# Layer 2 FFN results in a four-layer Macaron transformer kernel: update and norm of each sequence entered at set ticks of the next stage

## The chip, the cores and the metric

The kernel runs on one core of a Trainium2 chip. The metric is the device time of one execution in microseconds (us), as the median of several runs. All arithmetic is fp32. The engines are called as in the profile: PE (TensorE), DVE (VectorE), ACT (ScalarE), POOL (GpSimd) and SP (SyncE, which only issues transfers here).

## The reference

The input x holds 4 sequences of 512 tokens with 128 features. There are four layers, each a half-weighted FFN, an attention and the same FFN again, every one of them fed with a layer norm without weights:

```python
x = x + 0.5 * _L2_ffn_ref(_layernorm(x), L2_ffn_router_w, ...)
x = x + _L2_attn_ref(_layernorm(x), L2_attn_Wqkv, L2_attn_Wout)
x = x + 0.5 * _L2_ffn_ref(_layernorm(x), L2_ffn_router_w, ...)
x = x + 0.5 * _L3_ffn_ref(_layernorm(x), L3_ffn_wqkv, ...)
```

The layer 2 FFN is a mixture of eight experts: a router picks one expert for each token, which runs a gated two-layer network. The layer 2 attention has 16 heads and works in blocks. The layer 3 FFN is itself a small transformer of two layers with local attention over windows. The change lies at the two borders "first layer 2 FFN to layer 2 attention" and "second layer 2 FFN to layer 3 FFN", with a smaller piece at the first layer 0 FFN.

## The kernel before

x and y (the normed x) lie in SBUF as 128 tokens by 16 tiles by 128 features, four tiles (TB) to a sequence b. yT holds y turned, 128 features by 512 tokens for each sequence.

**Norms as chains.** The norm of a sequence has three parts. `statistics` (L196) makes four pairs of bn_stats and bn_aggr on DVE (L202, L205) and then `inverse_root`, eight small dependent operations (L184 to L190). `scaled` (L209) writes y in four operations (L214). `turn` (L236) has PE transpose the four tiles into a PSUM bank (`pt_y`, L161) and ACT copy it to yT (L241). So that this work needn't stand in one block, the kernel keeps chains. `chain(b)` opens a list for sequence b, and what is put into it is a part with a gap. `tick()`, which the loops of a stage call between their own parts, moves a clock on by one, and runs the next part of each chain whose gap has passed since the part before it. `leave_normed(b, spare, gap)` (L266) puts statistics, scale and, after a further gap, turn into a chain. `take(b)` (L289) runs what is left of b's chain at once and says whether y of b is ready; `begin_sequence(b)` (L297) is take, or else the whole norm on the spot.

**Order.** `tc.keep_in_program_order` pins an instruction among the pinned ones of its engine; the others are placed by a scheduler, which knows the dependencies and its own estimates of durations. Matmuls, transposes and many ACT instructions are pinned. In the kernel before, update, statistics and scale of the layer 2 FFN are not.

**Layer 2 FFN** (`l2_ffn`, L1211). The tokens are sorted into slots of 128, one expert for each slot, and the slots run through PE, ACT and DVE in a software pipeline; each slot's result is sent to a DRAM table od. Then, for each sequence, four indirect transfers issued on POOL fetch the rows of its tokens from od into y (L1327), and `update` (L1329, the DVE instruction is L1331) adds half of y to x. Update goes into the chain with gap 0, and leave_normed follows with gap 2. The tile pool of the stage is given back when all 16 transfers have landed, and the first tiles of the next stage are placed in that memory.

**Layer 2 attention** (`l2_attn`, L1351). A loop over n runs from -9 to 19, four n for each sequence; a table says at which n the parts of a sequence stand: stat at -9, scale at -8 and features (turn) at -7 ahead of the sequence's first n, each asking `take(b)` first, then projections k and q (`first` writes t at L1377, `second` at L1383), the keys km (L1394), the values v (L1409) and, from 0 on, scores s (L1429), their maximum (L1434) and a subtraction on POOL (L1435). The loop ticks once for each n below 0 and five times for each n from 0 on.

**Layer 3 FFN** (`l3_ffn`, L1549). Eight units (two inner layers by four sequences) of four steps each. A step projects q and k (`p_qk`, PE) and v, squares p_qk on ACT (sq), turns q and k by angle on DVE (t at L1611 and L1614), sums squares (rn, L1616), and on POOL adds the two t (L1618), takes an inverse root and scales (L1619). Later parts of a step run 2 to 6 steps behind: features, scores and their maximum (L1664, L1666), exponentials on ACT, products with sums on POOL (L1681), values. sq and the second t have one buffer each. `norm_unit` and `open_unit` fetch the sequence's norm two and one step ahead of a unit, and the loop, which begins at n = -2, ticks six times for each n.

**Layer 0 FFN** (`l0_ffn`, L331) ends with four updates of x (L479) out of one PSUM bank, which run one after the other.

Of the kernel before, what the change touches and what calls it, by code (L numbers as in the profile page):

```python
# [25 lines left out]
ALU = mybir.AluOpType  # L26
# [3 lines left out]
B, S, D, H, HD = 4, 512, 128, 16, 8  # L30
# [73 lines left out]
def tile_macaron(ctx, tc, x_in, const_in, vec_in, w0_in, ws_in, ws3_in, w2f_in, w3_in, out):  # L104
    nc = tc.nc
# [16 lines left out]
    def bank(tag, name):  # L122
        n = 2 if tag in "kqd" else 1
        return psum["pool"].tile([P, n * 512], F32, tag=tag, name=name, bufs=psum["bufs"][tag])

    x = keep.tile([P, NT, D], F32, name="x")
# [26 lines left out]
    y = keep.tile([P, NT, D], F32, name="y")  # L153
# [3 lines left out]
    def mm(dst, lhsT, rhs, start=True, stop=True):  # L157
        nc.tensor.matmul(dst, lhsT=lhsT, rhs=rhs, start=start, stop=stop)
# [7 lines left out]
    def transpose_in_order(dst, src):  # L166
        tc.keep_in_program_order(transpose(dst, src))
# [5 lines left out]
    def rows(ap, n):  # L173

        return ap[:, None, :].to_broadcast([ap.shape[0], n, ap.shape[1]])

    def inverse_root(sb, dst, src, name, op, c, eng=None):


        n = src.shape[-1]  # L180
        v = sb.tile([P, 3, n], F32, tag=name, name=name, bufs=2)
        eng = eng or nc.vector
        xx, yy, t = (v[:, i, :] for i in range(3))
        eng.tensor_scalar(xx, src, c, None, op)  # L184
        eng.tensor_scalar(yy.bitcast(I32), xx.bitcast(I32), -0.5, float(0x5F1FFFF9), ALU.mult, ALU.add)
        for to, a, b in ((yy, -0.703952253, 1.681913895), (dst, -0.50000016, 1.50000048)):
            eng.tensor_mul(t, yy, yy)
            if eng is nc.vector:
                eng.scalar_tensor_tensor(t, t, a, xx, ALU.mult, ALU.mult)
                eng.scalar_tensor_tensor(to, t, b, yy, ALU.add, ALU.mult)  # L190
            else:
                eng.tensor_mul(t, t, xx)
                eng.tensor_scalar(t, t, a, b, ALU.mult, ALU.add)
                eng.tensor_mul(to, t, yy)

    def statistics(src, b, eng=None, pinned=False):  # L196

        st = keep.tile([P, TB, 6], F32, tag="ln_st", name="ln_st", bufs=2)
        mv = keep.tile([P, TB, 2], F32, tag="ln_mv", name="ln_mv", bufs=3)
        r = keep.tile([P, TB], F32, tag="ln_r", name="ln_r", bufs=3)  # L200
        for t in range(TB):
            first = nc.vector.bn_stats(st[:, t, :], src[:, b * TB + t, :])  # L202
            if pinned and t == 0:
                tc.keep_in_program_order(first)
            nc.vector.bn_aggr(mv[:, t, :], st[:, t, :])  # L205
        inverse_root(keep, r, mv[:, :, 1], "ir4", ALU.add, 1e-5, eng)
        return mv, r

    def scaled(dst, src, b, stats):  # L209

        mv, r = stats
        for t in range(b * TB, b * TB + TB):
            i = t - b * TB
            nc.vector.tensor_scalar(dst[:, t, :], src[:, t, :], mv[:, i, 0:1], r[:, i : i + 1], ALU.subtract, ALU.mult)  # L214


    ordered = {"act": False}
# [1 line left out]
    def by_order(i):  # L219
        if ordered["act"]:  # L220
            tc.keep_in_program_order(i)
# [11 lines left out]
    def normalize(dst, src, b, pinned=False):  # L233
        scaled(dst, src, b, statistics(src, b, None, pinned))

    def turn(b):  # L236

        pt = bank("m", "pt_y")
        for t in range(TB):
            transpose_in_order(pt[:, ts(t, P)], y[:, b * TB + t, :])  # L240
        by_order(nc.scalar.copy(yT[:, b, :], pt))  # L241
# [6 lines left out]
    def chain(b):  # L248
        parts = deque()
        chains.append([b, clock[0], parts])  # L250
        return lambda gap, f, products=True: parts.append((gap, f, products))
# [11 lines left out]
                busy |= c[2][0][2]  # L263
                run(c)

    def leave_normed(b, spare, gap):  # L266

        st = []
        spare(1, lambda: st.append(statistics(x, b)), False)

        def scale():
            scaled(y, x, b, st[0])
            ready.add(b)

        spare(1, scale, False)
        spare(gap, lambda: turn(b))
        if routed:
            spare(1, lambda: logits(b))
# [4 lines left out]
    def finish_chains(b=None):  # L283
        while any(b in (None, c[0]) for c in chains):
            for c in reversed(list(chains)):
                if b in (None, c[0]):
                    run(c)

    def take(b):  # L289

        finish_chains(b)
        if b in ready:
            ready.discard(b)
            return True
        return False
# [32 lines left out]

    def l0_ffn(tag):  # L331
        with pool(tag) as sb:
            acc = sb.tile([P, 2, 4, 32], F32, name="acc")
            agg = sb.tile([64, 32], F32, name="agg")
# [139 lines left out]
            pb = bank("m", "pb")  # L474
            for b in range(B):
                mm(pb[:, ts(b, D)], selb[:, ts(b, P)], o4)
            for b in range(B):
                xb = x[:, ts(b, TB), :]
                nc.vector.scalar_tensor_tensor(xb, rows(pb[:, ts(b, D)], TB), 0.5, xb, ALU.mult, ALU.add)  # L479

# [718 lines left out]
    def logits(b):  # L1201

        nc.sync.dma_start(yd.rearrange("(p t) d -> p t d", t=NT)[:, ts(b, TB), :], y[:, ts(b, TB), :])
        pl = bank("m", "pl2")
        for t in range(TB):
            mm_in_order(pl[:, ts(t, 8)], yT[:, b, ts(t, P)], WS(ws, "2f_rw"))
        nc.vector.tensor_add(
            routed["g"][:, ts(b, TB), :], pl[:, : TB * 8].rearrange("p (t e) -> p t e", e=8), rows(VEC(vec, "2f_rb"), TB)
        )

    def l2_ffn(tag):  # L1211
        ready.clear()
        with pool(tag) as sb, banks(tag + "ps", a=2, g=2, t=2, m=2):
            l2_slots(sb)

    def l2_slots(sb):
        od = dram.tile([P * SLOTS, D], F32, tag="od", name="od")
        g = routed.pop("g")
        softmax8(sb, g)
# [4 lines left out]
        src = oh  # L1224
        for i in range(4):
            n, dst = 1 << i, cum[i % 2]
            nc.vector.tensor_copy(dst[:, :n, :], src[:, :n, :])
            nc.vector.tensor_add(dst[:, n:, :], src[:, n:, :], src[:, : NT - n, :])
            src = dst
# [95 lines left out]
        for b in range(B):  # L1325
            for i in range(b * TB, b * TB + TB):
                nc.gpsimd.indirect_dma_start(y[:, i, :], None, od[:, :], bass.IndirectOffsetOnAxis(ap=at[:, i : i + 1], axis=0))  # L1327

            def update(b=b):  # L1329
                xb, yb = x[:, ts(b, TB), :], y[:, ts(b, TB), :]  # L1330
                nc.vector.scalar_tensor_tensor(xb, yb, 0.5, xb, ALU.mult, ALU.add)  # L1331

            spare = chain(b)
            spare(0, update, False)
            leave_normed(b, spare, 2)

# [12 lines left out]
    def l2_attn(v4s):  # L1351
        pin = tc.keep_in_program_order
        with pool("l2a") as sb:
            stats, four, qk, kms, steps, ao, aoT = {}, {}, {}, {}, {}, {}, {}

            def stat(b):
                stats[b] = None if take(b) else statistics(x, b)

            def scale(b):
                if stats[b]:  # L1360
                    scaled(y, x, b, stats[b])

            def features(b):
                if stats[b]:
                    turn(b)

            def repeated(b):

# [105 lines left out]
            def output(b):  # L1474
# [6 lines left out]


            parts = [
                (stat, -9, 3), (scale, -8, 3), (features, -7, 3), (repeated, -4, 4),
                (lambda b: first(b, "k"), -6, 4), (lambda b: second(b, "k"), -5, 3),
                (lambda b: first(b, "q"), -5, 4), (lambda b: second(b, "q"), -4, 3),
                (lambda b: keys(b, (0, 1)), -4, 4), (lambda b: keys(b, (2, 3)), -3, 3),
# [5 lines left out]
            for n in range(-9, NT + 4):  # L1493
                for place, (part, lag) in enumerate(stages):
                    if part and 0 <= n - lag < NT:
                        part(n - lag)
                    for f, at, when in parts:
                        b, rest = divmod(n - at, TB)
# [333 lines left out]
    with pool("ws") as wp:  # L1832
        ws = wp.tile([P, WS.n], F32, name="ws")
        nc.sync.dma_start(ws, ws_in)
        with banks("ps0"), pool("l0x") as sb:
            tiles = attention0_tiles(sb)
            l0_ffn("l0f")
            l0_attn(tiles)
            l0_ffn("l0g")
        w3 = keep.tile([P, WA], F32, tag="wa", name="w3")  # L1840
        nc.sync.dma_start(w3[:, : W3.n], w3_in)
        with pool("l2x") as l2x:
            with pool("l1x") as xb:
                tiles, vms = attention_tiles(xb), linear_tiles(xb)
                v4s = attention2_tiles(l2x)
                for n in "wb":
                    nc.gpsimd.tensor_scalar_mul(VEC(vec, f"ln2{n}"), VEC(vec, f"ln2{n}"), 0.5)
                l1_ffn("l1f", xb, tiles)
                l1_attn(vms)
                routed["g"] = l2x.tile([P, NT, 8], F32, tag="g2f", name="g2f")  # L1850
                l1_ffn("l1g", xb, tiles)
                with banks("ps1", e=6, m=2):
                    finish_chains()
            l2_ffn("l2f")
            with banks("ps2"):
                routed["g"] = l2x.tile([P, NT, 8], F32, tag="g2f", name="g2f")
                l2_attn(v4s)
                finish_chains()
            l2_ffn("l2g")
    l3_ffn(w3, "l3f", True)  # L1860
    l3_attn()
    l3_ffn(w3, "l3g", False)
# [145 lines left out]
```

## Time and profile before

| what | value |
|---|---|
| median of 3 runs | 2889.82 us (2889.73 to 2892.66) |
| profiled execution | 2886.26 us; its span 2884.6 us |
| mean granted PE clock | 0.871 |
| PE, DVE, ACT, POOL busy | 78%, 62%, 43%, 32% of the span |
| first layer 2 FFN's gathers, first update to last | 1365.16 to 1380.21 us |
| first and second group of attention scores (L1429) | 1401.40 and 1409.99 us |
| end of layer 2 attention (last update of x, L1479) | 1499.70 us |
| second layer 2 FFN's gathers, first update to last | 1609.48 to 1624.31 us |
| layer 3 FFN: first p_qk on PE, first t (L1611) on DVE | 1633.33 and 1638.18 us |
| layer 3 FFN: L1618 of steps 0, 3, 5 and 10 on POOL | 1640.74, 1661.08, 1675.80, 1719.30 us |

The times in the rows are starts, counted from the start of the profiled execution's span. A line of a timeline gives start, duration, engine, source line, operation, what it writes and reads with shapes, how many equal ones are drawn together, and in brackets how long the engine had idled before it and what ended the wait. A line of windows gives, for a stretch, the busy time of each engine with its number of instructions, the granted PE clock as a share of full speed, and the share and rate of transfers.

### The profile page before, as it was taken

How to read it: one execution, taken by the hardware profiler on the slowest of the kernel's cores; microseconds unless marked ns; L12 is line 12 of the kernel's file. 1: busy time of each engine (PE TensorE's matmuls, PEld its weight loads, DVE VectorE, ACT ScalarE, POOL GpSimd, SP SyncE). 2: the span in 40 equal slices, each digit the busy share in tenths (PEclk: the TensorE clock that was granted, in tenths of full speed). 3: DMA queues.
4: the chain of work that ended last, by engine and by line, in shares of the span. 5: the costliest groups of instructions: out<-in, count | busy, mean ns of one | idle time of the engine just before them, and what ended most of it. 6: DMA issues, size and time to landing. Idle time of an engine off the chain costs nothing. (4 is left out here: it accounts for less than half of the span.)

```text
span 2884.6 us, 46981 instructions
## 1 busy us (share of the span) xinstructions
PE 2245.8 (78%) x17562; PEld 1171.8 (41%) x17562; DVE 1788.8 (62%) x4844; ACT 1243.1 (43%) x2678; POOL 911.9 (32%) x1704
## 2 busy tenths in 40 slices
PE   4387448988678899758668578997789998789987
PEld 2154123333343333347458455555322222455553
DVE  4745576775675677544754577776356554777763
ACT  3154214433333433313423277776134444567763
POOL 1022012233121231213313486774100000777661
PEclk8578659999887999869868799999689999899998
DMA  3052010000000000027007210000000000110000
GB/s 135 11 158 67 0 59 1 1 1 1 1 1 1 1 1 5 4 75 257 9 16 272 72 25 19 22 21 8 0 1 1 1 1 1 26 23 21 22 20 12
DMA packets 33772, 99.14 MB, mean 34 GB/s; under 512 B 6184, under 2 KB 12072, under 8 KB 33032
## 3 DMA queue, kind: packets, MB, share of 16 engines
q1 hardware_dynamic: 30616, 88.03, 9.4%
q0 software_dynamic: 2496, 5.12, 0.8%
q8 instruction: 139, 2.28, 0.3%
q10 hardware_dynamic: 432, 2.98, 0.3%
q14 instruction: 89, 0.73, 0.1%
HBM read 66.88 MB, written 14.55 MB: 28 GB/s over the span
## 5 line engine op out<-in xcount | busy, mean ns | idle before, releaser
L802 ACT ACTIVATE PT<-pk_at 128x1024 f32<-128x1024 f32 (+3 forms) x384 | 310.8, 809 | 543.9 <-PE pq_at L164 470.6
L164 PE MATMUL pk_at<-qx,km 32*128 32x512 f32 (+3 forms) x1536 | 368.1, 556 | 61.3 <-ACT PT L802 56.3
L164 PE MATMUL po_at<-PT,vh 128*32 128x512 f32 (+3 forms) x1536 | 328.7, 510 | 4.4 <-POOL PT L805 4.2
L772 DVE CUSTOM_DVE_ANT_0 s<-pq_at,cst 128x384 f32<-128x384 f32 (+3 forms) x512 | 248.4, 485 | 97.2 <-PE pq_at L164 85.8
L1563 ACT ACTIVATE s<-s,nm,rn 128x128 f32<-128x128 f32 x512 | 245.5, 482 | 2.1 <-DVE nm L1669 1.9
L805 POOL TENSOR_SCALAR_AFFINE_SELECT PT<-PT 128x256 f32<-128x256 f32 x256 | 106.8, 419 | 411.5 <-ACT PT L802 411.4
L164 PE MATMUL pq_at<-km,qT 32*128 32x384 f32 (+3 forms) x1024 | 225.2, 528 | 13.7 <-DVE nm L772 7.3
L164 PEld LDWEIGHTS pk_at<-qx,km 32*128 32x128 f32 x1536 | 119.7, 189 | 266.2 <-ACT PT L802 206.7
L767 DVE TENSOR_REDUCE nm<-pq_at 128x2 f32<-128x1024 f32 x128 | 156.2, 1225 | 104.4 <-PE pq_at L164 103.9
L1618 POOL TENSOR_TENSOR t<-t,t 128x1024 f32<-128x1024 f32 x64 | 151.3, 2364 | 132.1 <-DVE t L1614 131.7
L161 PE MATMUL pt_y<-ident,y 128*128 128x128 f32 x224 | 55.1, 376 | 157.6 <-DVE y L214 118.4
L164 PE MATMUL p_qk<-w,hT 128*128 128x512 f32 x256 | 146.5, 701 | 11.0 <-DVE t L1614 9.1
L164 PE MATMUL pq_at<-km,t 32*128 32x512 f32 x512 | 149.4, 689 | 7.0 <-DVE nm L767 4.9
L164 PEld LDWEIGHTS po_at<-PT,vh 128*32 128x32 f32 x1536 | 55.7, 109 | 222.2 <-issue 144.0
L161 PE MATMUL pt<-ident,s 128*128 128x128 f32 x640 | 92.2, 291 | 62.8 <-POOL s L1681 36.7
L241 ACT COPY yT<-pt_y 128x512 f32<-128x512 f32 x56 | 32.7, 584 | 242.8 <-PE pt_y L161 242.7
L1681 POOL TENSOR_TENSOR s<-s,sm 128x1024 f32<-128x1024 f32 x64 | 121.4, 1897 | 49.3 <-DVE sm L1680 41.2
L1611 DVE TENSOR_TENSOR t<-p_qk,w 128x1024 f32<-128x1024 f32 x64 | 78.3, 1223 | 71.7 <-ACT sq L1563 71.4
L1563 ACT ACTIVATE sq<-p_qk 128x1024 f32<-128x1024 f32 x64 | 65.5, 1023 | 127.7 <-PE p_qk L164 76.0
L161 PEld LDWEIGHTS pt<-ident,s 128*128 128x128 f32 x640 | 77.5, 149 | 95.2 <-POOL s L1681 51.5
L161 PEld LDWEIGHTS pt_y<-ident,y 128*128 128x128 f32 x224 | 35.0, 173 | 188.3 <-issue 119.0
L1305 DVE SCALAR_TENSOR_TENSOR hT<-pa,w,sg 128x128 f32<-128x128 f32 x184 | 51.8, 344 | 84.8 <-ACT sg L1304 63.7
(428 smaller groups left out, 5145.3 us busy)
## 6 DMA issues: line engine op xcount, KB each, us to landing
w<-in_w2f_dram SPq DMA_DIRECT2D x46, 836.0 KB, 5.9
vb<-v SPq DMA_DIRECT2D x112, 128.0 KB, 2.2
skew<-qe SPq DMA_DIRECT2D x16, 512.0 KB, 3.0
rel<-skew SPq DMA_DIRECT2D x64, 128.0 KB, 3.3
w<-in_w_dram SPq DMA_DIRECT2D x1, 4147.0 KB, 12.4
w<-in_w_dram SPq DMA_DIRECT2D x1, 3200.0 KB
od<-o SPq DMA_DIRECT2D x46, 64.0 KB, 5.0
yd<-y SPq DMA_DIRECT2D x8, 256.0 KB, 2.3
```

Source lines behind the costliest of these rows:

```text
L161: return nc.tensor.transpose(dst, src, ident[: src.shape[0], : src.shape[0]])
L164: tc.keep_in_program_order(nc.tensor.matmul(dst, lhsT=lhsT, rhs=rhs, start=start, stop=stop))
L241: by_order(nc.scalar.copy(yT[:, b, :], pt))
L767: nc.vector.tensor_reduce(to, pq.rearrange("p (i n) -> p i n", i=2), AX.X, ALU.max)
L772: nc.vector.tensor_tensor_reduce(s[:, :nk], pq[:, i * 512 : i * 512 + nk], causal[:, S - nk :], 1.0, -BIG, ALU.add, ALU.max, nm[:, qt, at ...
L802: by_order(nc.scalar.activation(PT[:, :, q0:], pk[:, :, q0:], AF.Exp, scale=SC8))
L805: nc.gpsimd.affine_select(d, d, pattern=[[0, 2], [1, P]], base=0, channel_multiplier=-1, compare_op=ALU.is_ge, fill=0.0)
L1305: nc.vector.scalar_tensor_tensor(hT[s][:, c, :], pa[:, ts(c, P)], b1[:, c : c + 1], sg, ALU.add, ALU.mult)
L1563: tc.keep_in_program_order(nc.scalar.activation(*args, **kw))
L1611: nc.vector.tensor_mul(by_head(t1), by_head(p3), over(tab[:, 0]))
L1618: nc.gpsimd.tensor_add(t1, t1, t2)
L1681: nc.gpsimd.tensor_mul(s, s, bcast(sm, P))
```

## The change

- The layer 2 FFN takes a tuple `ticks`. Update of sequence b enters its chain with gap ticks[b]: (0, 5, 8, 13) for the first FFN, (0, 13, 36, 60) for the second, where all were 0.
- Update and the four y operations of these chains are pinned in program order on DVE.
- The transfers of all sequences are issued in a loop of their own, ahead of the loop that makes the chains. Their order stays.
- The attention's stat, scale and features are replaced by one begin_sequence at -7.
- The first layer 0 FFN puts the updates of sequences 1 to 3 into their chains with gaps 2, 3 and 4; the second stays as it was.

```diff
-    def scaled(dst, src, b, stats):
+    def scaled(dst, src, b, stats, pinned=False):
...
-            nc.vector.tensor_scalar(dst[:, t, :], src[:, t, :], mv[:, i, 0:1], r[:, i : i + 1], ALU.subtract, ALU.mult)
+            s = nc.vector.tensor_scalar(dst[:, t, :], src[:, t, :], mv[:, i, 0:1], r[:, i : i + 1], ALU.subtract, ALU.mult)
+            if pinned:
+                tc.keep_in_program_order(s)
...
-    def leave_normed(b, spare, gap):
+    def leave_normed(b, spare, gap, pinned=False):
...
-            scaled(y, x, b, st[0])
+            scaled(y, x, b, st[0], pinned)
...
-    def l0_ffn(tag):
+    def l0_ffn(tag, chained):
...
-            for b in range(B):
+            def update(b):
                 xb = x[:, ts(b, TB), :]
                 nc.vector.scalar_tensor_tensor(xb, rows(pb[:, ts(b, D)], TB), 0.5, xb, ALU.mult, ALU.add)
+            for b in range(B):
+                if b and chained:
+                    chain(b)(b + 1, lambda b=b: update(b), False)
+                else:
+                    update(b)
...
+        for b in range(B):
             def update(b=b):
                 xb, yb = x[:, ts(b, TB), :], y[:, ts(b, TB), :]
-                nc.vector.scalar_tensor_tensor(xb, yb, 0.5, xb, ALU.mult, ALU.add)
+                tc.keep_in_program_order(nc.vector.scalar_tensor_tensor(xb, yb, 0.5, xb, ALU.mult, ALU.add))
             spare = chain(b)
-            spare(0, update, False)
-            leave_normed(b, spare, 2)
+            spare(ticks[b], update, False)
+            leave_normed(b, spare, 2, True)
...
             parts = [
-                (stat, -9, 3), (scale, -8, 3), (features, -7, 3), (repeated, -4, 4),
+                (begin_sequence, -7, 3), (repeated, -4, 4),
...
-            l0_ffn("l0f")
+            l0_ffn("l0f", True)
...
-            l0_ffn("l0g")
+            l0_ffn("l0g", False)
...
-            l2_ffn("l2f")
+            l2_ffn("l2f", (0, 5, 8, 13))
...
-            l2_ffn("l2g")
+            l2_ffn("l2g", (0, 13, 36, 60))
```

In the built order of the changed kernel, b0's norm still stands ahead of the next stage's own work. On DVE in the attention, b1's block stands behind the first k product, b2's and b3's around the first group of scores and ahead of the second group. In the layer 3 FFN, b1's stands between steps 0 and 1, b2's in steps 4 and 5, b3's in steps 8 and 9, and PE has the transposes of each ahead of the following step's p_qk.

More of the change, by code (lines that the diff above doesn't have):

```diff
@@ L1209, in logits, with l2_ffn, l2_slots @@
         )
-    def l2_ffn(tag):
+    def l2_ffn(tag, ticks):
         ready.clear()
         with pool(tag) as sb, banks(tag + "ps", a=2, g=2, t=2, m=2):
-            l2_slots(sb)
-    def l2_slots(sb):
+            l2_slots(sb, ticks)
+    def l2_slots(sb, ticks):
         od = dram.tile([P * SLOTS, D], F32, tag="od", name="od")
@@ L1353, in l2_attn @@
         with pool("l2a") as sb:
[L1354 to L1365, printed above, removed]
+            four, qk, kms, steps, ao, aoT = {}, {}, {}, {}, {}, {}
             def repeated(b):
```

## The prediction

> **What bounds the kernel now.** I read the page, then the idle time in front of the changed line L1331, then VectorE's timeline on both sides of it, then the windows of the stages that follow. The page says how much each engine does, and nothing of where:
>
> ```profile
> PE 2245.8 (78%) x17562; PEld 1171.8 (41%) x17562; DVE 1788.8 (62%) x4844; ACT 1243.1 (43%) x2678; POOL 911.9 (32%) x1704
> ```
>
> No engine is full over the span, so the two places must be read by themselves. L1331 is the update x += y/2; its idle time over both layer 2 FFNs:
>
> ```profile
> L1331 DVE SCALAR_TENSOR_TENSOR x<-y,x x8: 691/692/693, 1365.2 to 1624.3; 128x512 f32<-128x512 f32 x8
> its engine sat idle before it (us, times) until:
>   DMA y<-od,at: 26.0, 8
> ```
>
> All of it is a wait for gathers, which the change does not touch. VectorE around the first FFN's end (start, duration, instruction, idle before it and what ended that):
>
> ```profile
> 1375.05 0.69 DVE L1331 SCALAR_TENSOR_TENSOR x<-y,x 128x512 f32<-128x512 f32 x1 [2.79 <-DMA y<-od,at]
> ...
> 1376.01 1.19 DVE L214 TENSOR_SCALAR y<-x,ln_mv,ln_r 128x128 f32<-128x128 f32 x4
> ...
> 1380.21 0.69 DVE L1331 SCALAR_TENSOR_TENSOR x<-y,x 128x512 f32<-128x512 f32 x1 [3.00 <-DMA y<-od,at]
> ...
> 1386.63 1.11 DVE L214 TENSOR_SCALAR y<-x,ln_mv,ln_r 128x128 f32<-128x128 f32 x4
> 1387.66 0.68 DVE L1377 TENSOR_TENSOR t<-p,cst 128x512 f32<-128x512 f32 x1
> ```
>
> Between the last update (1380.21) and the attention's first own operation (1387.66) lie 7.45 us of norms of sequences that are not needed yet: that is what can be won. At the second FFN the like stretch runs from 1624.31 to the end of the norms at 1632.2, 7.9 us. What the work between costs when nothing else is on the engine is read at the end of the attention, update to norm:
>
> ```profile
> 1499.70 0.69 DVE L1479 TENSOR_TENSOR x<-po,x 128x512 f32<-128x512 f32 x1 [2.26 <-PE po L164]
> ...
> 1501.68 0.17 DVE L184 TENSOR_SCALAR ir<-ln_mv 128x4 f32<-128x4 f32 x1
> ...
> 1503.27 1.12 DVE L214 TENSOR_SCALAR y<-x,ln_mv,ln_r 128x128 f32<-128x128 f32 x4
> ```
>
> 1499.70 to 1504.39 is 4.7 us for one sequence, of which eight dependent small operations take 1.6. Where it has to go now is read from the windows (busy PE, PEld, DVE, ACT, POOL; clock; DMA):
>
> ```profile
> 1388.00:1400.00 12.00, 10.53 (x43) 6.20 (x42) 6.77 (x10) 5.27 (x9) 3.39 (x3) 0.85 0.00 0
> 1400.00:1410.00 10.00, 6.89 (x148) 4.86 (x148) 7.84 (x12) 6.51 (x9) 3.90 (x3) 0.77 0.01 2
> 1410.00:1420.00 10.00, 9.61 (x134) 6.73 (x134) 7.20 (x15) 3.90 (x9) 3.18 (x2) 0.89 0.01 2
> ```
>
> VectorE has idle time there, but it is short waits for PE's products, not a hole. In the layer 3 FFN, POOL is the bound from its first step; it goes from one step's work to the next without a gap while VectorE is some 1 to 3 us ahead:
>
> ```profile
> 1646.21 1.04 POOL L1619 TENSOR_TENSOR t<-t,rn 128x512 f32<-128x512 f32 x1
> 1647.21 2.36 POOL L1618 TENSOR_TENSOR t<-t,t 128x1024 f32<-128x1024 f32 x1
> ...
> 1673.94 1.90 POOL L1681 TENSOR_TENSOR s<-s,sm 128x1024 f32<-128x1024 f32 x1
> 1675.80 2.36 POOL L1618 TENSOR_TENSOR t<-t,t 128x1024 f32<-128x1024 f32 x1
> ```
>
> ```profile
> 1672.09 1.22 DVE L1611 TENSOR_TENSOR t<-p_qk,w 128x1024 f32<-128x1024 f32 x1 [0.70 <-ACT sq L1563]
> 1673.23 1.28 DVE L1614 TENSOR_TENSOR t<-p_qk,w 128x512 f32<-128x512 f32 x2
> ```
>
> The t of step 5 is ready at 1674.5, POOL takes it at 1675.80: a cushion of 1.3 us.
>
> **What the Trainium skill says.** "TensorE: Matmul & The Clock Gate", section on the architectural detail of the array: only weight loads are pulled ahead on PE, and VectorE and ScalarE are strict FIFOs; so a late instruction holds all behind it. The trace agrees (the transposes of y at L161 wait in line with the products). The same page, Part 1: PE runs at half clock after a few us of idleness and warms after some 3.4 us of work. It agrees: the four p_qk products took 3.62 us at 1658.01 after a pause and 1.95 at 1666.60. "SBUF — State Buffer", section on the two separate sides: VectorE's two-port operations and GpSimd lock each other out for a whole instruction. It agrees:
>
> ```profile
> 1441.69 2.50 DVE L214 TENSOR_SCALAR y<-x,ln_mv,ln_r 128x128 f32<-128x128 f32 x3
> ```
>
> Three y operations took 2.50 us beside a POOL subtraction (1441.95, 1.91 long), where four took 1.12 alone.
>
> **The change part by part.** No arithmetic, transfer or queue entry is added or removed: the two orders have equal instruction counts, SP's is the same, and POOL's 16 gathers still stand first and in the same order. Moved are, for sequences 1 to 3 of both FFNs, update, norm, four transposes with their ScalarE copy.
>
> *Start of the attention.* Its first tile (t of L1377) waits in the changed order for all gather queues, so it cannot start before 1380.2; it stands behind b0's norm alone, whose inputs landed at 1365. Gain: 1387.66 − 1380.3 = 7.3 us.
>
> *What is given back there.* Ahead of the second group of scores (s, L1429, 1409.99 before) now lie three blocks of 4.7 us, 14.1 in all. Before, VectorE did 6.77 + 7.84 + 0.3 = 14.9 us of work from 1387.66 to there. With no idle time at all it would get there at 1380.3 + 14.9 + 14.1 = 1409.3, 0.7 us earlier: the lower bound, and no gain of 7. Walked in order: the first scores come at about 1400.2 (1401.40 before), since b1's block fits partly into waits for cold products. Then y(b2) waits for POOL's subtraction, PE holds the next q product behind y(b2)'s transposes, then y(b3) (some 1413.5) ahead of the first values of b1 (2 us cold), and the second scores come at about 1417.5, 7.5 us later: the upper bound. The truth lies where part of the 7.4 us of old idle time is used; from there on the order is the old one, and VectorE's 28% of idle time in the last window gives back a little. I take +4.5, between −1 and +7.5.
>
> *Start of layer 3.* p_qk of step 0 goes from 1633.33 to about 1625.4, −7.9. b1's block stands between step 0 and step 1 on VectorE and its transposes ahead of p_qk(1) on PE, which then runs cold (3.6). I get L1618 of step 1 at 1645.9 against 1647.21, and −1.8 at most from step 2 on: 6 of the 7.9 are spent.
>
> *b2 and b3 in layer 3.* b2's block falls into steps 4 and 5, b3's into 8 and 9, where POOL has no gap. Lower price: 4.7 + some waiting of the dependent operations, less the 1.3 cushion and about 1 of idle time used: 2.5 us each. Upper: p_qk of the next step stands behind the transposes on PE, so the chain is y, transposes 0.5 + 1.65, p_qk 3.6 (cold), square 1.0, t 2.4; t of step 5 comes to some 1682 where it was 1674.5; from −1.8 that is up to 7.8 us for each. I take 4.7 each. Sum: −1.8 + 9.4 = +7.6, between +3.2 and +13.8. Why it isn't given back: POOL is the bound behind it, and has no idle time to catch up with until step 11.
>
> *Layer 0.* Updates of sequences 2 and 3 leave the front of b0's norm only in part: they are not pinned, and in the changed order both still stand ahead of y(b0). One statistics pair and two small operations go: −0.4, ±0.5.
>
> *Pinning of y.* Costs nothing itself; it forbids filling b0's window, already cheap. 0.
>
> **Sum**, against the profiled execution of 2886.26 us (span 2884.6): +4.5 + 7.6 − 0.4 = +11.7, 2898.0. That execution lies 3.6 below the median of 2889.82, so the median becomes 2901.5. The mechanism's own range: −1 + 3.2 − 0.9 = +1.3 to 7.5 + 13.8 + 0.1 = +21.4, so 2891 to 2911.
>
> **Rivals.** *Covered*, the one on the other side: the norms drop into waits that VectorE has anyway, and the earlier starts stay. For it: VectorE idles 20 to 30% in all these windows and 5.49 us before step 0 of layer 3. It decides if PE's transposes of b1 to b3 find y ready when PE gets there, that is, if a block of 4.7 us costs under 2.5 us (7.3 + 7.9 gained, six blocks to pay). At the most −7.3 − 7.9 − 0.4 = −15.6, 2874; with a third of it paid, −10.4, 2879. Against: the floor of 1409.3 in the attention, where even perfect packing leaves −0.7. A later recovery there would have to come from the idle time after 1410. *Half and half*: attention gets back to −4 by its end, where all engines idle (PE busy 50 to 80%), layer 3 pays +4: 2889.5. *Nothing happens* because a scheduler keeps the old order: excluded, the built order shows the blocks moved.
>
> **How the numbers follow.** Chances: paid for (my forecast) 0.63, of which 0.03 falls under the bound of 0.2%, which is 5.8 us and about what a measurement of this kernel can tell from no change; half and half 0.10; covered 0.27. So faster 0.27, same 0.13, slower 0.60. The range reaches from 2878 (leaving out about half of the covered case) to 2911 (the upper sum).
>
> **What would show it.** In the profile after: t of L1377 at 1380 to 1381 (start kept); s of L1429's second group after 1412 (paid); y beside a POOL operation at 2 us or more; p_qk of step 0 near 1625.5; L1618 of step 3 about 2 us early, of step 5 some 2 to 3 late, of step 9 some 5 to 10 late. Wrong would be the forecast if L1618 of steps 5 and 9 kept their −7.9, or the attention's end came 5 us early: then blocks are cheaper than their length, because they run in waits.

## The result and the profile after

The changed kernel takes 2924.11 us (2918.40 to 2935.74, 4 runs) against 2891.24 us (2889.73 to 2894.17, 4 runs) of the kernel before beside it: a ratio of 1.0118, 95% interval 1.0084 to 1.0151, some 33 us slower. In a second comparison (run all_parts below) it was 1.0103, from 1.0079 to 1.0127. Slower was forecast, but 2901.5 with an upper end of 2911: the direction held, the size did not. Even all the upper prices of the forecast together, +21.4 us, are too small. The profiled execution took 2926.87 us, with a span of 2925.2.

The page says as little of where as before; all the work is the same:

```profile
PE 2258.8 (77%) x17562; PEld 1177.2 (40%) x17562; DVE 1803.1 (62%) x4844; ACT 1243.8 (43%) x2678; POOL 916.2 (31%) x1704
```

So I compared the starts of equal instructions in both traces. What the changed kernel is late by grows in three places: 7.0 us at the end of layer 1 (around 1205 us), where the program is the same; 10.3 us in the layer 2 attention; 20.5 us in the layer 3 FFN. The first is dealt with last. Lateness in a stage is given below without what was there at its start: 9.9 us before the attention (the 7.0, and smaller pieces near it), 20.2 before layer 3. It counts from the gathers, so "start 7 early" is against those.

VectorE in the attention (start, duration, instruction, and in brackets the idle time before it and what ended it):

```profile
1378.65 1.12 DVE L214 TENSOR_SCALAR y<-x,ln_mv,ln_r 128x128 f32<-128x128 f32 x4
1390.46 0.69 DVE L1380 TENSOR_TENSOR t<-p,cst 128x512 f32<-128x512 f32 x1 [10.69 <-DMA y<-od,at]
1391.07 0.68 DVE L1345 SCALAR_TENSOR_TENSOR x<-y,x 128x512 f32<-128x512 f32 x1
...
1397.64 2.06 DVE L214 TENSOR_SCALAR y<-x,ln_mv,ln_r 128x128 f32<-128x128 f32 x4
...
1411.37 1.42 DVE L1432 TENSOR_TENSOR s<-ps_2a,cst 128x256 f32<-128x256 f32 x4 [0.26 <-PE ps_2a L164]
...
1413.96 2.70 DVE L214 TENSOR_SCALAR y<-x,ln_mv,ln_r 128x128 f32<-128x128 f32 x4
...
1424.46 1.12 DVE L214 TENSOR_SCALAR y<-x,ln_mv,ln_r 128x128 f32<-128x128 f32 x4
...
1429.24 1.42 DVE L1432 TENSOR_TENSOR s<-ps_2a,cst 128x256 f32<-128x256 f32 x4 [0.70 <-PE ps_2a L164]
```

The first t stands at 1390.46 where the gathers let it: 1390.46 − 9.9 = 1380.6 against 1387.66, 7.1 us early, as forecast. Ahead of it VectorE is idle for 10.69 us; before, statistics of sequences 1 and 2 and y of sequence 0 ran in that time. The first scores (1411.37) are 0.1 us late, the second (1429.24) 9.4. Two y groups take 2.06 and 2.70 us instead of 1.12, each beside work of POOL. What that does to PE is seen in its own timeline:

```profile
1398.99 1.25 PE L161 MATMUL pt_y<-ident,y 128*128 128x128 f32 x4 [4.05 <-DVE y L214]
...
1414.44 0.30 PE L161 MATMUL pt_y<-ident,y 128*128 128x128 f32 x1 [3.06 <-DVE y L214]
1416.20 0.99 PE L161 MATMUL pt_y<-ident,y 128*128 128x128 f32 x3 [1.46 <-DVE y L214]
...
1424.86 1.25 PE L161 MATMUL pt_y<-ident,y 128*128 128x128 f32 x4 [4.25 <-DVE y L214]
```

All four lines are PE's transposes of y of sequences 1 to 3, and in front of them it stood still for 4.05, 3.06, 1.46 and 4.25 us, 12.8 together, with the next products behind them in its order. Windows around the second group of scores (busy PE, PEld, DVE, ACT, POOL; clock; transfers):

```profile
1412.00:1429.00 17.00, 8.85 (x90) 6.42 (x90) 11.97 (x33) 7.72 (x11) 3.58 (x2) 0.60 0.00 1
1429.00:1439.00 10.00, 9.61 (x159) 6.53 (x140) 7.93 (x16) 3.89 (x8) 3.15 (x2) 1.00 0.01 2
```

From 1412 to 1429 no engine is full, and the granted clock is 0.60: the engines wait for each other in turn. From 1429, where no norms are in the way, PE is at 9.61 of 10 again.

The layer 3 FFN shows it more plainly. First PE ahead of steps 1, 5 and 9; then VectorE, with the first and last line from the blocks of sequences 1 and 3 and the others from around step 5; then POOL, whose L1621 is L1618 of before, in steps 0, 1, 4 and 5, and L1684 at two places:

```profile
1660.66 1.16 PE L161 MATMUL pt_y<-ident,y 128*128 128x128 f32 x4 [9.39 <-DVE y L214]
...
1695.93 0.48 PE L161 MATMUL pt_y<-ident,y 128*128 128x128 f32 x1 [9.12 <-DVE y L214]
1697.79 0.99 PE L161 MATMUL pt_y<-ident,y 128*128 128x128 f32 x3 [1.38 <-DVE y L214]
1698.57 3.57 PE L164 MATMUL p_qk<-w,hT 128*128 128x512 f32 x4
...
1741.71 1.16 PE L161 MATMUL pt_y<-ident,y 128*128 128x128 f32 x4 [11.23 <-DVE y L214]
```

```profile
1654.51 1.99 DVE L1345 SCALAR_TENSOR_TENSOR x<-y,x 128x512 f32<-128x512 f32 x1
...
1694.92 3.33 DVE L214 TENSOR_SCALAR y<-x,ln_mv,ln_r 128x128 f32<-128x128 f32 x4
...
1703.28 1.22 DVE L1614 TENSOR_TENSOR t<-p_qk,w 128x1024 f32<-128x1024 f32 x1 [3.42 <-ACT sq L1566]
...
1739.36 1.82 DVE L190 SCALAR_TENSOR_TENSOR ln_r<-ir 128x4 f32<-128x4 f32 x1
```

```profile
1653.62 2.34 POOL L1621 TENSOR_TENSOR t<-t,t 128x1024 f32<-128x1024 f32 x1 [7.05 <-DVE t L1617]
...
1668.81 2.35 POOL L1621 TENSOR_TENSOR t<-t,t 128x1024 f32<-128x1024 f32 x1 [8.37 <-DVE t L1617]
...
1689.32 2.35 POOL L1621 TENSOR_TENSOR t<-t,t 128x1024 f32<-128x1024 f32 x1
...
1695.76 1.89 POOL L1684 TENSOR_TENSOR s<-s,sm 128x1024 f32<-128x1024 f32 x1
1705.84 2.37 POOL L1621 TENSOR_TENSOR t<-t,t 128x1024 f32<-128x1024 f32 x1 [8.19 <-DVE t L1617]
...
1739.27 1.90 POOL L1684 TENSOR_TENSOR s<-s,sm 128x1024 f32<-128x1024 f32 x1
```

PE waits 9.39 us for y of sequence 1, 9.12 and 1.38 for that of sequence 2, and 11.23 for that of sequence 3. It runs cold, that is at a lower granted clock (0.51 from 1698 to 1702), behind that of sequence 2 (p_qk 3.57 us, where it took 1.95 in the kernel before). Then t follows at 1703.28 after VectorE itself has waited 3.42 us for ACT's square of p_qk, and POOL, which had no gap before, is left without work for 8.19 us at step 5 and 8.37 at step 1. Without the 20.2 us of the start: step 0 is 7.3 early, step 1 1.4 late, step 3 1.2 late, step 5 9.8 late, step 10 20.9 late.

The late blocks are also longer than 4.7 us, as operations of them meet POOL. In sequence 1's the update takes 1.99 us instead of 0.69 and y 1.83 instead of 1.12; in sequence 2's y takes 3.33; in sequence 3's three of the eight small operations take 1.11, 1.01 and 1.82 us where they take 0.16 or 0.17 elsewhere, and the last of them, shown above, ends at 1741.18 with POOL's L1684. That is 2.0, 2.2 and 3.5 us more, 7.7 together.

### The profile page after: what moved, and what is told of

Its sections match the earlier page's. It is cut to its first block, busy times and chain, and to the rows that moved or that the text cites. A ratio compares the mean times of both kernels' runs of the same rounds, so it can differ in the third digit from the quotient of the medians.

```text
span 2925.2 us, 46973 instructions
## 1 busy us (share of the span) xinstructions
PE 2258.8 (77%) x17562; PEld 1177.2 (40%) x17562; DVE 1803.1 (62%) x4844; ACT 1243.8 (43%) x2678; POOL 916.2 (31%) x1704
## 4 chain that ended last, share of the span: by engine, by line
PE 51%; DVE 23%; ACT 10%; POOL 8%; issue 6%; DMA 1%; SPq 0%; POOLq 0%; DVEq 0%; ACTq 0%
PE pk_at L164 10%; PE po_at L164 6%; ACT PT L811 4%; PE pa L164 3%; PE pag L164 3%; PE po L164 3%; PE pe L164 3%; PE p_qk L164 2%; DVE t L1617 2%; DVE t L1614 2%; PE pg L164 2%; DVE y L1021 2%; POOL t L1621 2%; PE pq_at L164 2%; PE pv L164 2%
## 5 line engine op out<-in xcount | busy, mean ns | idle before, releaser
L1621 POOL TENSOR_TENSOR t<-t,t 128x1024 f32<-128x1024 f32 x64 | 151.4, 2366 | 151.0 <-DVE t L1617 150.8
L1684 POOL TENSOR_TENSOR s<-s,sm 128x1024 f32<-128x1024 f32 x64 | 121.5, 1898 | 49.0 <-DVE sm L1683 40.6
```

The costliest lines, as they stand in the source:

```text
L1621: nc.gpsimd.tensor_add(t1, t1, t2)
L1684: nc.gpsimd.tensor_mul(s, s, bcast(sm, P))
```

## The experiments

The theory after the traces: **a block of update, statistics and y that comes late on VectorE holds PE, which has the transposes of y in line ahead of products it could do**; the bounding engine behind them starves. Its rival: VectorE's 14 us of displaced work costs its length wherever it stands. A second question is which part of the change puts the block there, the ticks or the pinning.

Stage losses in the tables are again read from equal instructions in two traces: from the end of the layer 2 FFN to the end of the attention, and from there to the middle of the layer 3 FFN. They come from one execution each and hold to about 3 us.

| run | ratio to before, 95% | attention | layer 3 FFN |
|---|---|---|---|
| all_parts (the changed kernel) | 1.0103 (1.0079 to 1.0127) | +10.4 | +20.4 |
| p_l0 | 0.9991 (0.9978 to 1.0004) | 0 | 0 |
| p_l2f | 1.0026 (1.0008 to 1.0045) | +10.1 | +2.2 |
| p_l2g | 1.0059 (1.0034 to 1.0085) | +0.7 | +20.8 |
| no_l0 | 1.0104 (1.0076 to 1.0132) | +7.6 | +20.6 |
| late_turn | 1.0038 (1.0019 to 1.0056) | +3.3 | +8.8 |
| turn_only | 0.9969 (0.9958 to 0.9980) | −3.8 | −2.6 |
| pin_update | 1.0075 (1.0057 to 1.0092) | +3.9 | +20.4 |
| pin_y | 1.0009 (1.0000 to 1.0019) | +3.2 | −0.2 |
| in_gather | 0.9994 (0.9982 to 1.0007) | +0.6 | −5.7 |
| unpinned | 0.9947 (0.9926 to 0.9967) | −5.7 | −3.8 |
| unp_late | 0.9942 (0.9925 to 0.9959) | −9.3 | −5.2 |

**One part at a time.** Layer 0 alone, that is the layer 0 lines of the change on the kernel before:

```diff
-            l0_ffn("l0f")
+            l0_ffn("l0f", True)
```

> The layer 0 part alone, on the kernel before. In the trace of the changed kernel the stages after layer 0 run 3.3 us early and lose this between 650 and 720 us, and 9 us more are lost at the end of layer 1 (1198 to 1213 us), where the program has the same instructions. If the small shift of layer 0 causes both by the granted PE clock there, this kernel is some 5 to 10 us slower than before and its clock at the end of layer 1 is near 0.63. If the loss there is chance of one execution, or has another cause, it is within 3 us of before.

Measured: no difference that can be told. It is no slower, though its profiled execution lost 7 us at the end of layer 1 as that of the changed kernel did; see the last section. The part is worth nothing, and neither the gain of 0.4 us that was forecast nor a loss shows.

The first layer 2 FFN alone, as the changed kernel with the rest put back (layer 0's updates at once too):

```diff
-            l2_ffn("l2g", (0, 13, 36, 60))
+            l2_ffn("l2g", (0, 0, 0, 0), False)
```

> The first layer 2 FFN's part alone (ticks 0, 5, 8, 13, pinned, begin_sequence in the attention), the other two parts as before. Both theories, PE held by the transposes of y in its order, and VectorE's 14 us of displaced work, expect what the changed kernel's trace shows for this stage: +10 us, from 8 to 12, and nothing elsewhere. If the stages interact, it is another number.

The second alone, in the same way (False stands for not pinned):

```diff
-            l2_ffn("l2f", (0, 5, 8, 13))
+            l2_ffn("l2f", (0, 0, 0, 0), False)
```

(with stat, scale and features back in the attention, too)

> The second layer 2 FFN's part alone (ticks 0, 13, 36, 60, pinned), the others as before. Expected from the changed kernel's trace: +21 us, from 18 to 24, in three pieces of about 8.6 (from a start 7.2 early to 1.4 late by step 1), 8.7 (step 5) and 11 (step 9). If half of the changed kernel's loss were due to a clock that the other parts set off, it is under 12.

Each does in its stage what the changed kernel does there, 10.1 and 20.8 us, and little elsewhere. The ratios sum to 0.85%, 25 us; the two comparisons of the whole gave 1.18 and 1.03%, with intervals that reach down to 0.84 and 0.79. As far as these tell, the parts add up.

The whole beside a version without layer 0's part:

> The changed kernel itself, beside the next run on the same chip. The two layer 2 parts alone gave ratios of 1.0026 and 1.0059. If the parts add up and nothing else is slow, the ratio is about 1.0085, some 25 us. If they set each other off, it is near the 1.0118 of the first measurement. In its profile the end of layer 1 (about 1198 us) shows whether the 8.5 us lost there with the same instructions come again.

> The changed kernel without the layer 0 part (all four updates at once again). Layer 0 alone gave 0.9991, from 0.9978 to 1.0004. If it is worth nothing here either, this kernel is within 4 us of the run beside it; if the shift of layer 0 brings the loss at the end of layer 1, it is 8 us faster than that.

The two agree, 1.0103 and 1.0104, each to within 0.003. Layer 0 does not set off any loss that shows.

**PE's order: late_turn.** The transposes of y are put a few ticks further back, and nothing else is changed in the program (the second tuple holds the gaps):

```diff
-            leave_normed(b, spare, 2, True)
+            leave_normed(b, spare, gaps[b], True)
...
-            l2_ffn("l2f", (0, 5, 8, 13))
+            l2_ffn("l2f", (0, 5, 8, 13), (2, 2, 6, 16))
...
-            l2_ffn("l2g", (0, 13, 36, 60))
+            l2_ffn("l2g", (0, 13, 36, 60), (2, 8, 8, 8))
```

> The changed kernel with nothing moved but the transposes of y and their copies: gaps of the turn 2, 2, 6, 16 at the first layer 2 FFN and 2, 8, 8, 8 at the second, where all were 2, so that on PE they stand behind the next products. VectorE's order stays nearly the same. If PE's waits for y in its order make the loss, the attention loses at most 4 instead of 10 and the layer 3 FFN about 7 instead of 21: some 17 us faster than the changed kernel, 2900 to 2908. If VectorE's displaced work makes it, it stays within 5 us of the changed kernel, 2919 to 2929.

2906.14 us, in the range that the theory gave: 19 of the 31 us are gone. In the attention VectorE's instructions stand in the same order as in the changed kernel, so the 7 us gone there come from PE's order (and ACT's copies). In layer 3 the scheduler has moved VectorE's unpinned work too: t of steps 1, 5 and 9 now goes ahead of part of the norm next to it. So the 12 us gone there are not PE's order alone, though in the changed kernel t of steps 1 and 5 waited 3.4 us each, with the norm done, for ACT's square of a p_qk that PE made late. PE in layer 3, at what is still in front of the transposes of sequences 2 and 3:

```profile
1682.45 1.24 PE L161 MATMUL pt_y<-ident,y 128*128 128x128 f32 x4 [8.38 <-DVE y L214]
...
1722.12 1.15 PE L161 MATMUL pt_y<-ident,y 128*128 128x128 f32 x4 [4.75 <-DVE y L214]
```

8.38 and 4.75 us are left of 10.5 and 11.23, and in front of sequence 1's PE waits 10.68 us, no less than before: even later in its order y is not there when PE comes. So a wait does not cost its length; it matters which products stand behind it. The rest, +3.3 and +8.8, is what the block costs by itself or through these waits; this run does not part them.

**Only VectorE's order put back: turn_only.** PE's order is that of the changed kernel to the last row of both stages; updates (not pinned here) and norms stand early, as before:

```diff
-            leave_normed(b, spare, 2, True)
+            leave_normed(b, spare, gaps[b])
...
-            l2_ffn("l2f", (0, 5, 8, 13))
+            l2_ffn("l2f", (0, 0, 0, 0), (2, 20, 9, 14))
...
-            l2_ffn("l2g", (0, 13, 36, 60))
+            l2_ffn("l2g", (0, 0, 0, 0), (2, 14, 37, 61))
```

> VectorE as in the kernel before (updates and norms at tick 0, unpinned), while PE keeps the changed kernel's order, with the transposes of sequences 1 to 3 between the next stage's products. If the place of the transposes in PE's order costs by itself, some of the changed kernel's +31 stays, 5 us or more. If they cost only because y is late when PE gets to them, this kernel is within 3 us of before: VectorE's block of norms ahead of each stage is there again, and with it the late start.

It is 0.3% faster than before (2882.31 against 2889.94 us), which neither expectation had. The place of the transposes costs nothing; it is even of use. A likely reason is that the first products of each stage no longer stand behind 16 transposes: before, PE waited 6.25 us for sequence 1's norm at 1627.93, ahead of p_qk of step 0, which now starts 3.3 us sooner after the gathers. The same order of PE makes 31 us of loss with late norms and a gain with early ones.

**Which pin: pin_update, pin_y, unpinned.** Ticks as in the changed kernel:

```diff
# pin_update: y not pinned
-            leave_normed(b, spare, 2, True)
+            leave_normed(b, spare, 2)
# pin_y: update not pinned
-                tc.keep_in_program_order(nc.vector.scalar_tensor_tensor(xb, yb, 0.5, xb, ALU.mult, ALU.add))
+                nc.vector.scalar_tensor_tensor(xb, yb, 0.5, xb, ALU.mult, ALU.add)
# unpinned: both
```

> The changed kernel with only the updates pinned, y not. The statistics can't come ahead of their update, so the whole block of 4.7 us stays inside the next stage, and y's place is almost that of the changed kernel. If the late block is the cause, the loss stays for the most part: 20 to 33 us over before. If pinning y is what does it, it is within 5 us of before or faster.

> The changed kernel with only y pinned, the updates not. The built order has all four updates and most of the statistics ahead of the next stage or in its first waits; inside the stage there are only the four y operations of a sequence, 1.1 us. If the late block (statistics and their eight dependent operations ahead of y) is the cause, this kernel loses little: between 8 us faster than before and 4 slower. If y's place alone makes PE wait, it is 10 us or more over before.

> The changed kernel, ticks and all, but update and y are not pinned. In the built order the scheduler then puts all four updates ahead of the next stage, and most of the norms too, and only single y operations between the next stage's steps. If the loss is the blocks' place on VectorE and what PE waits for because of it, this one loses nothing and keeps a part of the earlier starts: 2 to 10 us faster than before. If the ticks alone make the loss, wherever the scheduler puts the work, it stays near the changed kernel.

PE's order is the changed kernel's in all three. With the update pinned the loss of layer 3 is whole (+20.4), VectorE's order there is the changed kernel's too, and PE waits 9.48, 10.5 and 11.22 us. With y alone pinned it is gone (−0.2): the update leads the whole chain, and held at its tick it holds the sixteen statistics and small operations behind it. In the attention, where the operations around are pinned too, both pins cost: +3.9 with the update's, +3.2 with y's, +10.4 with both. With neither, the scheduler does by itself what the ticks were to do, and the kernel is 15 us faster than before, more than the 2 to 10 expected. VectorE of the unpinned kernel at the border to layer 3:

```profile
1605.36 0.69 DVE L1345 SCALAR_TENSOR_TENSOR x<-y,x 128x512 f32<-128x512 f32 x1 [0.63 <-DMA y<-od,at]
...
1610.44 0.69 DVE L1345 SCALAR_TENSOR_TENSOR x<-y,x 128x512 f32<-128x512 f32 x1 [2.93 <-DMA y<-od,at]
...
1615.32 0.69 DVE L1345 SCALAR_TENSOR_TENSOR x<-y,x 128x512 f32<-128x512 f32 x1 [2.60 <-DMA y<-od,at]
1615.93 1.11 DVE L214 TENSOR_SCALAR y<-x,ln_mv,ln_r 128x128 f32<-128x128 f32 x4
...
1622.12 0.69 DVE L1345 SCALAR_TENSOR_TENSOR x<-y,x 128x512 f32<-128x512 f32 x1
...
1623.07 1.10 DVE L214 TENSOR_SCALAR y<-x,ln_mv,ln_r 128x128 f32<-128x128 f32 x4
...
1625.78 0.34 DVE L214 TENSOR_SCALAR y<-x,ln_mv,ln_r 128x128 f32<-128x128 f32 x1
1626.86 1.23 DVE L1616 TENSOR_TENSOR t<-p_qk,w 128x1024 f32<-128x1024 f32 x1 [0.74 <-ACT sq L1568]
```

Three updates stand in the waits for gathers, the fourth and y of sequences 0 and 1 ahead of the first t, and the rest goes one or two y at a time between the steps. POOL in steps 1 to 3 has no gap:

```profile
1635.96 2.36 POOL L1623 TENSOR_TENSOR t<-t,t 128x1024 f32<-128x1024 f32 x1
...
1642.73 2.35 POOL L1623 TENSOR_TENSOR t<-t,t 128x1024 f32<-128x1024 f32 x1
...
1649.70 2.35 POOL L1623 TENSOR_TENSOR t<-t,t 128x1024 f32<-128x1024 f32 x1
```

So VectorE's displaced work does not cost its length wherever it stands, as the rival has it: with the same order on PE it makes a loss of 31 us in late blocks, and none here, where it is early or in small pieces.

pin_y lost more than unpinned; in its trace y, in one piece of four, still falls beside POOL's work (3.15 us at 1669.30), and PE stands 5.58 us in front of it.

**Versions meant to be faster: in_gather, unp_late.** in_gather stays pinned, with sequences 0 to 2 in the gathers' time (the second tuple holds the gaps of the transposes, as in late_turn):

```diff
-            l2_ffn("l2f", (0, 5, 8, 13))
+            l2_ffn("l2f", (0, 0, 1, 7), (2, 2, 2, 16))
-            l2_ffn("l2g", (0, 13, 36, 60))
+            l2_ffn("l2g", (0, 0, 1, 9), (2, 11, 11, 4))
```

> Changed kernel with other ticks, (0, 0, 1, 7) and (0, 0, 1, 9), and turn gaps (2, 2, 2, 16) and (2, 11, 11, 4): norms of sequences 0 to 2 are done while VectorE waits for gathers anyway, and only sequence 3's stands in the next stage, in a stretch where VectorE waits for cold products, with its transposes behind those products. If a norm costs only where VectorE has no wait to put it in and where PE is held by it, both earlier starts stay for the most part: attention -3 to -6, layer 3 FFN -4 to -7, together some 10 us faster than before, 2884 of 2894. If any norm moved behind the stage's start costs its length, it is within 3 us of before.

Layer 3 gains 5.7, within what was expected, the attention nothing (+0.6), which was not. In its trace all three updates stand ahead of y of sequence 0, which comes only 3.8 us behind the third of them (1380.13, 1383.89), all twelve y in 3.17 us. As a whole it is like the kernel before, and the 10 us expected did not come.

unp_late is unpinned with the gaps of late_turn:

> Nothing pinned, the changed kernel's ticks, and the later transposes of late_turn. In the unpinned kernel PE still waits 0.9 us for y in the attention and loses 2.7 us at step 5 of the layer 3 FFN. If PE's waits behind y make that, this kernel is 2 to 4 us faster than unpinned, about 17 to 20 under before. If that is VectorE's work, it is within 2 us of unpinned.

0.9942 against 0.9947, each to within 0.002: not to be told from unpinned. The stage columns, of one execution each, have it 5 us better; the times don't bear that out. Both beat both kernels: some 15 us under the one before, 45 under the changed one.

## Why the prediction was wrong

**Start of the attention and of layer 3: right.** −7.3 and −7.9 were forecast, −7.1 and −7.3 measured. **Layer 0: no effect,** as far as can be told. **The kind of loss: right**; y late, PE behind it, cold products, POOL starved, each step named in the forecast is in the trace. That the kernel came out slower is not luck, then; that it came out this much slower was missed.

**The size failed in three terms.**

*"What is given back there" (attention): taken +4.5, measured +10.3.* The walk in order came near: second scores 7.5 late forecast, 9.4 measured. But I called the walk an upper bound and went 3 us down from it, towards a floor of VectorE's work with no idle time. That idle time could not be used. In the stretch of the second scores VectorE is busy for 11.97 of 17 us, and PE, on which it waits, stands behind y itself. And "gives back a little" was nothing: 9.4 us late at 1429, 10.3 at the end.

*"Start of layer 3": 6 of the 7.9 us forecast as spent from step 2 on, measured 8.5* (from 7.3 early in step 0 to 1.2 late in step 3). Of the 2.4 us between, 2.0 can be POOL's, beside which the update and y of sequence 1 took longer.

*"b2 and b3 in layer 3": taken 4.7 each, measured 8.6 (steps 3 to 5) and 11.1 (to step 10).* The lower price, 2.5, was the error of the attention once more: a cushion of 1.3 us and idle time of VectorE, in a place where the chain runs through PE. The chain that I gave as the upper price, 7.8, is the one in the trace, but one term is missing from it. I had shown that y beside POOL takes longer, cited "SBUF — State Buffer" for it, and put it at nothing here. In sequence 3's block three small operations took 3.5 us longer beside POOL, which is about what 11.1 is over 7.8. In sequence 2's y took 2.2 us longer, and that was hidden by an error the other way: the links from the end of y to the end of t, 9.15 us in the forecast, took 7.4, as most of the transposes' time did not come on top. That t of step 5 came 3.5 us later than forecast (1685.5 against 1682) is mostly what the start had already lost.

The 7.7 us of POOL in layer 3 are read from durations in one trace (the second one of the changed kernel, all_parts, has the same); no run takes them away and leaves the rest.

Together −1.8 + 9.4 = +7.6 became +20.5, and the +12.1 for the two stages together became +31 (28 to 31 in the three executions with both parts).

**The rival "covered"** had its point of decision right, that y be ready when PE gets there, and turn_only and unpinned are the kernels where it is. What I did not see is that the pin of the update decides this. I priced y's pin alone ("Costs nothing itself") and left the update's out; with the update's alone the whole loss of layer 3 is there, with y's alone none of it. None of that stage's own work on VectorE is pinned, so the pin does more than keep pinned instructions in order among themselves, as I had described it: in the traces an unpinned update and its statistics stand where its data arrive, and a pinned one at its tick. Why the scheduler does so was not looked into.

**Open:** how the rest of late_turn (+12 us) divides between VectorE's time and PE's waits; and how much of the loss POOL's collisions and the cold clock each make. None of this was tried. On the clock, the forecast's own pair of p_qk shows two speeds and not what sets them: the 3.62 us at 1658.01 followed a pause of 2.31 us and the 1.95 us at 1666.60 one of 2.20.

## What to carry to other kernels

Work that only waits for data should be free to run when the data come; a pin on the first link of a chain (here one 0.7 us update, at a late tick) holds all that hangs on it, and is dear where another engine has the end of the chain in line ahead of work it could do. When an order is fixed by hand, price it along the chain through the engine that stands behind it, not by the idle time of the engine that runs the moved work, and look at every operation of it for what POOL does at that time. Where a walk in program order and a count of busy time give different ends, take the walk as the estimate: here even it was too short.

## What the runs showed of the hardware

**A clock that differs between executions at the same instructions.** Around 1205 us, in the end of layer 1, PE has the same instructions in all kernels. The kernel before, and p_l0 (same columns as the windows above):

```profile
1200.00:1210.00 10.00, 8.61 (x49) 4.14 (x48) 5.26 (x18) 1.58 (x4) 1.22 (x3) 1.00 0.00 0
```

```profile
1200.00:1210.00 10.00, 10.00 (x44) 4.55 (x43) 0.69 (x1) 1.94 (x4) 1.38 (x4) 0.50 0.00 0
```

The granted clock is 1.00 in the one and 0.50 in the other, with PE busy for 8.61 and all 10 us, and p_l0 comes out of it 7 us later. In p_l0 PE is busy for all of the 10 us before this window too, also at 0.50: that it warms after some 3.4 us of work, as the forecast took it, did not hold here, and the measurement decides. Six of the fourteen profiled executions have this loss: the first of the changed kernel, p_l0, turn_only, pin_update, pin_y and unp_late lose 5 to 7 us there, the others nothing there. Among these others is all_parts, which is the changed kernel itself. So the program doesn't set it, but what does is not shown. It means that two profiled executions can differ by 7 us in one place for no reason of the program, and that stages have to be compared one by one.

**The price of VectorE's collisions with POOL.** Four y operations took 1.11 to 1.12 us alone, and 2.06, 2.70, 3.15 and 3.33 where POOL worked beside them. A short operation can pay far more than its own length: the 0.16 us operation at 1739.36 took 1.82, and the 0.17 us one at 1734.09 took 1.11. In these cases VectorE's operation ended within 0.1 us of POOL's. So a short operation took about as long as the rest of the POOL operation that it met.
